# A state-space scan kernel: some input products moved from VectorE and GpSimd to ScalarE, with a transpose by TensorE, and the steps' side work placed by tables

## The chip, the cores and the metric

The kernel runs on one NeuronCore of a Trainium2 chip. The core has five engines that run side by side, each through its own queue in order: TensorE (PE in the profile; its weight loads are PEld), VectorE (DVE), ScalarE (ACT), GpSimd (POOL) and SyncE (SP), which only issues DMAs here. Tiles lie in SBUF or in PSUM[...]. The metric is the time of one execution in microseconds (us), the median of three runs.

## What is computed

Four layers in one launch; only layers 0 and 1 contain the work that changes. Each is a selective state-space scan over images of 56 x 56 positions, in four directions (by rows, by columns, and both backwards). For each direction, channel and state n of 16, with the position i running in order:

```
def step(state, inp):
    u_i, d_i, b_i, c_i = inp
    dA = jnp.exp(d_i[..., None] * A)
    state = dA * state + (d_i * u_i)[..., None] * b_i[:, :, None, :]
    y = jnp.einsum('bkdn,bkn->bkd', state, c_i)
    return (state, y)
```

So for a state n the kernel needs a decay exp(delta * A[n]), an input product (delta * u) * B[n], in which B[n] is one row of numbers shared by all channels, a recurrence along the positions, a product with the row C[n], and the sum of these products over the 16 states. Layer 0 has two images one after the other with 256 channels (two halves of 128); layer 1 has both images side by side on 128 partitions (64 channels each) and goes through four heads one after the other, each needing the one before. Layers 2 and 3 (attention, a long convolution, a mixture of experts) follow and are not touched.

## The kernel before

The 3136 positions are cut into four pieces of 784 (`QT`). A *group* is one direction and one piece; there are 16 in a scan run. A *step* s is one state of one group and one half of the channels: in layer 0 a group has 2 x 16 steps, in layer 1 16. Layer 0 has two runs of 512 steps, layer 1 four of 256, so there are 2048 steps. Between the runs lie stages with norms, projections and convolutions.

One step uses every engine, on tiles of 128 x 784:

- `decay` (L339): ScalarE writes `a` = exp(A[n] * delta) into one of two PSUM slots (`pdec0`, `pdec1`, by the parity of s). A slot is free when the scan two steps earlier has read it.
- The input product. For 11 of 16 states (*direct* below), `spread` (L364) lets TensorE copy the row B[n] to all 128 partitions of a PSUM tile `b`, of which there is one, and VectorE multiplies it by `du` = delta * u (L417). For the five states in `POOLED` (2, 5, 8, 11, 14) the row comes by a broadcast DMA (`on_all`, L299) and GpSimd multiplies (L433).
- `scan` (L358): one VectorE instruction, h = a * h + input along the 784 positions, in place in `h`; from the second piece of a direction on it starts from a carried state, which `keep` (L350) copies out on ScalarE.
- GpSimd multiplies `h` by the row C[n], which comes by a broadcast DMA (L430, result `p`).
- `add_up` (L378): TensorE adds `p` to the group's PSUM sum `acc` with two matmuls; `take_out` (L398) copies the full sum to `y` on ScalarE in the third step of the next 16.

All of it is written out by hand: `emit(s)` issues the pieces of several steps in one fixed order, so that in iteration s the scan of step s, the decay and product of step s+1, the spread of s+2, the DMA for C of s+3 and the sum of step s-2 stand together. The queues keep that order:

```
        if one:
            self.decay(one)
```

Beside the steps runs the *preparation* of the next group (`pieces_of`): `rows` (projection on TensorE, copied by ScalarE), `keep`, `fetch`, `band`, `rest`, `store` and `spread` (the rows of B go through DRAM and are split into three bf16 parts, `rest` on GpSimd L195), `steps` and `soft` (delta, with a change of the activation table), `copy` and `times` (du; L223 on VectorE). A list gives each piece an iteration and a place in it. Pieces of place 0 use the same single PSUM tile `b` (pool `prow`) as `spread`. `first` does the preparation of a run's first group in the stage before the run.

## Time and profile before

| what | value |
|---|---|
| time, median of three runs | 9113.85 us (9098.83 to 9114.19) |
| span of the profiled execution | 9096.6 us |
| its six scan runs together | 5060.4 us |
| VectorE busy over the span | 7088.0 us, 78% |
| GpSimd busy over the span | 6350.1 us, 70% |
| ScalarE busy over the span | 3854.8 us, 42% |
| TensorE busy over the span | 7993.2 us, 88% (pipelined, not a measure of its peak) |

The page gives no time of the profiled execution other than its span; the three runs lie from 2 to 17 us above it. In a group's row, "L358 DVE ... x1536 | 2791.8, 1840 | 51.6 <-ACT a L339 28.7" means: line 358 of the kernel, on VectorE, 1536 instructions, busy 2791.8 us in all and 1840 ns each, and VectorE was idle for 51.6 us just before them, 28.7 of it until ScalarE had written `a`. Shares over the whole span mix stages with different limits, so the scan runs are best read by themselves. In a row of stretches, each engine's busy time stands ahead of its number of instructions, and the last three columns are TensorE's granted clock (1 is full), the share of the DMA engines' time and the bandwidth.

### The profile page before, as it was taken

To read this page: it belongs to the slowest core of one execution; us is meant where nothing else is said; L and a number is where in the kernel's file an instruction comes from. 1 tells how busy PE (TensorE), PEld (TensorE's weight loads), DVE (VectorE), ACT (ScalarE), POOL (GpSimd) and SP (SyncE) were. 2 spreads that over 40 slices of the span, in tenths; PEclk is the share of its full clock that TensorE was granted. 3 is DMA by queue.
4 is the path that set the end of the run, shared out by engine and by line. 5 is a ranking of instruction groups with operands and counts; after the bars stand their busy time and mean duration, and the time that the engine had idled before them with its cause. 6 is when DMAs were issued, how large, how long until landed. Compare 5 with 4: busy or idle time off the path is not lost. (4 is left out here: it accounts for less than half of the span.)

```text
span 9096.6 us, 93496 instructions
## 1 busy us (share of the span) xinstructions
PE 7993.2 (88%) x28687; PEld 4765.5 (52%) x28687; DVE 7088.0 (78%) x7568; ACT 3854.8 (42%) x6644; POOL 6350.1 (70%) x4066
## 2 busy tenths in 40 slices
PE   8888888888887888888888888699999999999998
PEld 4444445444444444444444444355688888874555
DVE  8999998999997997998999899511467667665442
ACT  4555545555555555554554555433211111114331
POOL 6999996999996997998899799566311111115551
PEclk9999999999999998998999899799999999999999
DMA  5666664666664995996898699100233333320004
GB/s 159 221 221 220 222 212 127 221 221 220 222 220 110 230 226 134 227 228 157 203 227 204 157 227 224 39 3 3 85 96 105 104 94 110 93 63 8 14 1 135
DMA packets 780368, 1362.92 MB, mean 150 GB/s; under 512 B 133101, under 2 KB 405486, under 8 KB 779834
## 3 DMA queue, kind: packets, MB, share of 16 engines
q1 hardware_dynamic: 779866, 1356.95, 53.1%
q8 instruction: 227, 3.72, 0.2%
q14 instruction: 275, 2.25, 0.1%
HBM read 1317.03 MB, written 39.60 MB: 149 GB/s over the span
## 5 line engine op out<-in xcount | busy, mean ns | idle before, releaser
L430 POOL TENSOR_TENSOR p<-h,c 128x784 f32<-128x784 f32 x2048 | 3761.2, 1864 | 115.0 <-DVE h L358 33.1
L358 DVE TENSOR_TENSOR_SCAN h<-a,state,h 128x784 f32<-128x784 f32 x1536 | 2791.8, 1840 | 51.6 <-ACT a L339 28.7
L378 PE MATMUL acc<-p,center 128*128 128x392 f32 x4096 | 1499.0, 499 | 22.7 <-POOL p L430 20.8
L378 PE MATMUL acc<-p,ident 128*128 128x392 f32 x4096 | 1491.9, 498 | 6.7 <-POOL p L430 6.7
L417 DVE TENSOR_TENSOR h<-du,b 128x784 f32<-128x784 f32 x1408 | 1336.7, 949 | 75.6 <-PE b L364 70.4
L339 ACT ACTIVATE a<-delta,L0A 128x784 f32<-128x784 f32 x1024 | 939.3, 918 | 973.4 <-DVE h L358 971.5
L339 ACT ACTIVATE a<-delta,L1A 128x784 f32<-128x784 f32 x1024 | 939.2, 917 | 908.3 <-DVE h L358 905.3
L364 PE MATMUL b<-three,sel 96*128 96x512 bf16 (+1 forms) x2816 | 728.6, 341 | 563.9 <-DVE h L417 460.1
L433 POOL TENSOR_TENSOR h<-du,b 128x784 f32<-128x784 f32 x640 | 1190.3, 1860 | 4.1 <-PE pcv L460 4.1
L378 PEld LDWEIGHTS acc<-p,center 128*128 128x128 f32 x4096 | 740.9, 192 | 536.8 <-POOL p L430 60.2
L378 PEld LDWEIGHTS acc<-p,ident 128*128 128x128 f32 x4096 | 743.9, 192 | 512.8 <-POOL p L430 26.5
L1089 POOL TENSOR_TENSOR total<-total,e 128x448 f32<-128x448 f32 (+1 forms) x644 | 735.6, 1142 | 326.0 <-ACT e L1078 286.0
L358 DVE TENSOR_TENSOR_SCAN h<-a,h 128x784 f32<-128x784 f32 x512 | 901.7, 1780 | 36.7 <-ACT a L339 21.1
L364 PEld LDWEIGHTS <-sel 96*128 96x128 bf16 x2816 | 281.5, 100 | 1230.9 <-issue 1048.6
L1572 DVE TENSOR_TENSOR u<-u,cv 128x512 f32<-128x512 f32 x1024 | 623.7, 681 | 326.6 <-PE cv L1559 325.4
L1603 POOL TENSOR_TENSOR u<-u,S 128x1024 f32<-128x1024 f32 x64 | 150.0, 2365 | 1041.0 <-DVE S L1572 1041.0
L1078 ACT ACTIVATE e<-sc 128x448 f32<-128x448 f32 (+1 forms) x700 | 377.2, 543 | 723.0 <-PE sc L1076 596.3
L1574 ACT COPY u<-cv 128x512 f32<-128x512 f32 x256 | 149.5, 587 | 829.3 <-PE cv L1559 775.7
L1673 PE MATMUL pj<-u,Wm 128*128 128x196 f32 (+8 forms) x1536 | 354.7, 384 | 5.7 <-DVE A L1679 5.7
L1076 PE MATMUL sc<-big 128*128 128x448 f32 (+1 forms) x700 | 323.4, 547 | 15.4 <-ACT e L1078 12.3
L1070 PE MATMUL av<-e,big 128*128 128x448 f32 (+1 forms) x700 | 320.9, 545 | 1.2 <-DVE e L1083 1.0
L1653 POOL TENSOR_TENSOR both<-mpm 128x512 f32<-128x512 f32 x32 | 40.6, 1269 | 392.3 <-DVE Wm L1709 272.8
(452 smaller groups left out, 11251.1 us busy)
## 6 DMA issues: line engine op xcount, KB each, us to landing
c<-rows SPq DMA_DIRECT2D x1024, 392.0 KB, 4.0
c<-rows SPq DMA_DIRECT2D x2048, 196.0 KB, 4.8
b<-rows SPq DMA_DIRECT2D x320, 392.0 KB, 4.5
b<-rows SPq DMA_DIRECT2D x640, 196.0 KB, 4.6
H<-raw SPq DMA_DIRECT2D x32, 1568.0 KB, 7.6
wC<-win SPq DMA_DIRECT2D x64, 576.0 KB, 6.4
w<-in_L_weight_dram SPq DMA_DIRECT2D x52, 512.0 KB, 6.3
wA<-win SPq DMA_DIRECT2D x64, 384.0 KB, 5.6
```

The source lines that it names most:

```text
L339: self.k.nc.scalar.activation(x["a"], g["delta"][ci], AF.Exp, scale=self.w["A"](g["kd"], ci, x["n"]))
L358: self.k.nc.vector.tensor_tensor_scan(h, a, h, start, ALU.mult, ALU.add)
L364: self.k.nc.tensor.matmul(ps[:, c0:c1], lhsT=self.w["selB"](x["n"]), rhs=x["g"]["three"][:, c0:c1], start=True, stop=True)
L378: nc.tensor.matmul(job["acc"][:, i, 0:392], lhsT=self.w["sum"], rhs=x["p"][:, 392 * i : 392 * (i + 1)], start=False, stop=n == NS - 1,)
L417: nc.vector.tensor_tensor(one["h"], one["g"]["du"][one["ci"]], one["b"], ALU.mult)
L430: nc.gpsimd.tensor_tensor(now["p"], now["h"], now["c"], ALU.mult)
L433: nc.gpsimd.tensor_tensor(three["h"], three["g"]["du"][three["ci"]], three["b"], ALU.mult)
L1076: nc.tensor.matmul(ps[:n], lhsT=keys[b][:, KT * j : KT * j + n], rhs=q, start=True, stop=True)
L1078: nc.scalar.activation(e[:n], ps[:n], AF.Exp, scale=scale)
L1089: nc.gpsimd.tensor_tensor(total[:n], total[:n], e[:n], ALU.add)
L1572: nc.vector.tensor_tensor(place(o), place(o), ps, ALU.add)
L1673: nc.tensor.matmul(ps[:, lo - c0 : hi - c0], lhsT=Ws[f][:, eo, r, :], rhs=u[:, b, f, lo - a0 : hi - a0], start=f == 0, stop=f == 1,)
```

## The change

A third way to make the input product joins the two. For *turned* states (1, 5, 7, 11, 13 in layer 0; 3 and 11 in layer 1) ScalarE works on transposed tiles. The group's `du` is transposed once (`turn`: seven tiles of 112 positions by 128 channels, through PSUM, into `duT`), and so are the rows of B (`across`, into `BT`). With positions on the partitions, B[n] is one number per partition, so a `fan` is an activation Copy of one 112 x 128 tile with a scale per partition; seven of them make a state's product in layer 0, 14 of 64 columns in layer 1, where the two images have rows of their own. `back` lets TensorE transpose the seven tiles into the PSUM slot that the decay would have used, and the decay of a turned state goes to an `h` tile in SBUF instead; the scan then reads `a` from SBUF and the product from PSUM, and writes `h` over `a`.

Fewer states are pooled (3, 9, 15 in layer 0; 1, 6, 9, 14 in layer 1), and 8 (layer 0) or 10 (layer 1) stay direct. `copy` becomes a ScalarE copy into PSUM in place of a TensorE product with the identity. Tables now say in which iteration each fan (`fans`, by the six iterations before the scan), each sum (`adds`, how many per iteration) and each preparation piece (`lists`, with `short` while the first group of layer 1 runs) is issued. The transposed tiles lie in memory that is otherwise idle in the runs; for that, layer 1's `hT` becomes a small rotating tile.

```diff
-POOLED = (2, 5, 8, 11, 14)
 HALF = QT // 2
+TS = QT // TP
...
+        self.pooled, self.turned = w["pooled"], w["turned"]
+        self.duT, self.bT = w["turn"][0:2], w["turn"][2:]
...
+                i = len(self.groups)
+                self.groups.append(dict(
+                    kd=kd, q=q, step=step, back=back,
+                    duT=[self.duT[(i * self.nch + ci) % 2] for ci in range(self.nch)],
+                ))
...
-            g["copy"] = product(ps, [0, 1], lambda m: k.ident, [xq[ci]])
+            g["copy"] = ps[:, :, 0:HALF]
+            nc.scalar.copy(g["copy"], part(xq[ci], [0, 1]))
...
+        def transposed(out, of, n, tiles, ps):
+            ps = ps.rearrange("p i c -> p (i c)")[:TP]
+            for i, j in enumerate(tiles):
+                nc.tensor.transpose(ps[:, n * i : n * (i + 1)], of[0:n, TP * j : TP * (j + 1)], k.ident[0:n, 0:n])
+            nc.scalar.copy(
+                out[:, tiles[0] : tiles[-1] + 1], ps[:, 0 : n * len(tiles)].rearrange("p (i c) -> p i c", c=n)
+            )
+
+        def across(ps):
+            g["BT"] = once("BT", 32 * TS)[:TP]
+            transposed(g["BT"].rearrange("p (i c) -> p i c", c=32), g["xd"], 32, range(TS), ps)
+
+        def turn(ci, ps, tiles=range(TS)):
+            transposed(g["duT"][ci], g["du"][ci], 128, tiles, ps)
...
+        f["across"](ps())
+        for ci in range(self.nch):
+            for i in range(0, TS, 3):
+                f["turn"](ci, ps(), range(i, min(i + 3, TS)))
...
-        def bands(keep, fetch, band, apart, store, spread):
-            yield from ((keep, 2, "keep"), (fetch, 2, "fetch"), (store, 2, "store"), (spread, 2, "spread"))
-            for i in range(3):
-                yield band + apart * i, 2, "band", i
...
+        lists = self.w["short"] if short and self.nch == 1 else self.w["lists"]
...
+        self.fans, self.adds = {}, self.w["adds"]
+        for i, x in enumerate(x for x in steps if x["n"] in self.turned):
+            x["bT"] = self.bT[i % len(self.bT)]
+            todo = [(x, j, *part) for j in range(TS) for part in self.w["parts"]]
+            at = self.w["fans"]
+            for j, count in enumerate(at.get(x["s"] % 32, at[None])):
+                self.fans.setdefault(x["s"] - 6 + j, []).extend(todo[:count])
+                todo = todo[count:]
...
-            if place == 0:
+            if place < 2:
...
+    def fan(self, x, i, c0, c1, row):
+
+
+        g, r = x["g"], 32 * i + row + x["n"]
+        self.k.nc.scalar.activation(
+            x["bT"][:, i, c0:c1], g["duT"][x["ci"]][:, i, c0:c1], AF.Copy, scale=g["BT"][:, r : r + 1]
+        )
+
+    def slot(self, x, at=0):
+        return self.pa[x["s"] % 2].tile([128, 1024], F32, name=f"a{x['s'] % 2}")[:, at : at + QT]
+
+    def back(self, x):
+
+        x["b"] = self.slot(x, 512 - 4 * TP)
+        for i in range(TS):
+            self.k.nc.tensor.transpose(x["b"][:, TP * i : TP * (i + 1)], x["bT"][:, i, :], self.k.ident[:TP, :TP])
+
+    def direct(self, x):
+        return x["n"] not in self.pooled and x["n"] not in self.turned
+
     def decay(self, x):
         g, ci = x["g"], x["ci"]
-        x["a"] = self.pa[x["s"] % 2].tile([128, 1024], F32, name=f"a{x['s'] % 2}")[:, 0:QT]
+        if x["n"] in self.turned:
+            x["a"] = x["h"] = self.hp.tile([128, QT], F32, name="h")
+        else:
+            x["a"] = self.slot(x)
...
         self.k.nc.scalar.activation(x["a"], g["delta"][ci], AF.Exp, scale=self.w["A"](g["kd"], ci, x["n"]))
...
+        b = x["b"] if n in self.turned else h
         start = 0.0 if g["step"] == 0 else self.state[g["kd"], g["step"] - 1, ci][:, n : n + 1]
         if g["back"]:
-            a, h = a[:, ::-1], h[:, ::-1]
-        self.k.nc.vector.tensor_tensor_scan(h, a, h, start, ALU.mult, ALU.add)
+            a, h, b = a[:, ::-1], h[:, ::-1], b[:, ::-1]
+        self.k.nc.vector.tensor_tensor_scan(h, a, b, start, ALU.mult, ALU.add)
...
+    def add(self, s):
+        for _ in range(self.adds[s % len(self.adds)]):
+            if self.sums and "acc" in self.sums[0]["job"]:
+                self.add_up(self.sums.pop(0))
...
+        if done:
+            self.sums.append(done)
...
-        if one:
+        if one and one["n"] not in self.turned:
             self.decay(one)
...
+        if two and two["n"] in self.turned:
+            self.decay(two)
+        for args in self.fans.get(s, ()):
+            self.fan(*args)
+        if one and one["n"] in self.turned:
+            self.back(one)
+        self.prepare(s, 1)
+        if one and self.direct(one):
             one["h"] = self.hp.tile([128, QT], F32, name="h")
             nc.vector.tensor_tensor(one["h"], one["g"]["du"][one["ci"]], one["b"], ALU.mult)
-        if two and two["n"] not in POOLED:
+        if two and self.direct(two):
             self.spread(two)
+        soon = self.w["soon"] and (s, 0) in self.pieces
+        if soon:
+            self.add(s)
...
         self.prepare(s, 0)
         if now:
...
-        if done:
-            self.sums.append(done)
-            if done["n"] == 2:
-                self.begin_sum(done["job"])
-            elif done["n"] > 2:
-                for _ in range(2 if done["n"] in (6, 9, 12) else 1):
-                    self.add_up(self.sums.pop(0))
+        if done and done["n"] == 2:
+            self.begin_sum(done["job"])
+        if not soon:
+            self.add(s)
...
+                "parts": ((0, 128, 0),),
+                "pooled": (3, 9, 15),
+                "turned": (1, 5, 7, 11, 13),
+                "adds": (0, 2, 0, 0, 0, 1, 1, 2, 1, 1, 1, 0, 1, 1, 2, 0, 3, 0, 2, 0, 1, 0, 2, 1, 2, 1, 0, 1, 2, 1, 1, 2),
+                "soon": True,
+                "fans": {
+                    None: (0, 2, 2, 2, 1, 0),
+                    1: (0, 2, 2, 1, 2, 0),
+                    5: (2, 3, 2, 0, 0, 0),
+                    7: (0, 0, 0, 7, 0, 0),
+                    11: (1, 3, 3, 0, 0, 0),
+                    13: (3, 3, 0, 1, 0, 0),
+                    17: (0, 2, 1, 3, 1, 0),
+                    21: (0, 3, 3, 1, 0, 0),
+                    23: (3, 4, 0, 0, 0, 0),
+                    27: (0, 0, 1, 2, 0, 4),
+                    29: (0, 0, 0, 5, 2, 0),
+                },
+                "lists": [
+                    [
+                        (1, 0, "rows", [0]), (3, 0, "rows", [1]), (3, 2, "keep"), (5, 0, "across"),
+                        (5, 2, "fetch"), (8, 2, "band", 0), (8, 2, "rest", 0), (10, 2, "band", 1),
+                        (10, 2, "rest", 1), (11, 0, "steps", 0, [0, 1]), (15, 0, "steps", 1, [0, 1]),
+                        (18, 2, "band", 2), (21, 2, "soft", 0), (21, 2, "soft", 1), (23, 2, "store"),
+                        (25, 2, "spread"), (25, 0, "copy", 0), (25, 2, "times", 0), (27, 0, "turn", 0),
+                        (29, 0, "copy", 1), (29, 2, "times", 1), (41, 0, "turn", 1),
+                    ],
+                ],
+                "turn": [X[:, TS * i : TS * (i + 1), 1, :] for i in range(4)],
...
+            "parts": ((0, 64, 0), (64, 128, NS)),
+            "pooled": (1, 6, 9, 14),
+            "turned": (3, 11),
+            "adds": (0, 2, 2, 0, 0, 1, 2, 1, 1, 1, 1, 2, 1, 1, 1, 0, 3, 1, 0, 0, 0, 1, 2, 1, 1, 1, 2, 0, 1, 1, 1, 1),
+            "soon": False,
+            "fans": {
+                None: (0, 4, 4, 4, 2, 0),
+                3: (0, 10, 4, 0, 0, 0),
+                11: (4, 0, 1, 7, 2, 0),
+                19: (4, 5, 5, 0, 0, 0),
+                27: (5, 1, 3, 2, 3, 0),
+            },
+            "lists": [
+                [
+                    (1, 0, "rows", [0, 1]), (2, 2, "keep"), (4, 0, "steps", 0, [0, 1]), (5, 2, "fetch"),
+                    (9, 0, "across"), (9, 2, "band", 0), (9, 2, "rest", 0), (10, 2, "band", 1),
+                    (10, 2, "rest", 1), (11, 2, "band", 2), (17, 2, "soft", 0), (19, 2, "store"),
+                    (22, 2, "spread"), (23, 0, "copy", 0), (23, 2, "times", 0), (25, 0, "turn", 0),
+                ],
+                [
+                    (12, 0, "rows", [0, 1]), (14, 2, "keep"), (15, 0, "steps", 0, [0, 1]), (17, 2, "soft", 0),
+                    (19, 2, "fetch"), (20, 0, "across"), (27, 2, "band", 0), (27, 2, "rest", 0),
+                    (28, 0, "copy", 0), (28, 2, "times", 0), (29, 2, "band", 1), (29, 2, "rest", 1),
+                    (31, 2, "band", 2), (33, 2, "store"), (35, 2, "spread"), (39, 0, "turn", 0),
+                ],
+            ],
+            "short": [
+                [
+                    (1, 0, "rows", [0, 1]), (4, 2, "keep"), (4, 0, "steps", 0, [0, 1]), (5, 2, "fetch"),
+                    (6, 2, "soft", 0), (7, 0, "across"), (7, 2, "band", 0), (7, 2, "rest", 0),
+                    (7, 2, "times", 0, False), (8, 2, "band", 1), (8, 2, "rest", 1), (9, 2, "band", 2),
+                    (9, 2, "store"), (10, 2, "spread"), (12, 0, "turn", 0),
+                ],
...
+            "turn": [
+                big[5][:TP, 128 * TS * i : 128 * TS * (i + 1)].rearrange("p (i c) -> p i c", c=128) for i in range(3)
+            ],
...
-            nc.scalar.copy(self.hT[:, cs], pt)
+            hT = sp.tile([2 * D, CH], F32, name="hT")
+            nc.scalar.copy(hT, pt)
             ps = vp.tile([128, CH], F32, name="pcv")
-            nc.tensor.matmul(ps, lhsT=W["in_w"][:, 0, :], rhs=self.hT[:, cs], start=True, stop=True)
+            nc.tensor.matmul(ps, lhsT=W["in_w"][:, 0, :], rhs=hT, start=True, stop=True)
```

## The prediction

> **What bounds it now.** I read the page's groups first, then the stretches of the six scan runs, then a few microseconds of VectorE and GpSimd in order of time. A scan run here goes from its first to its last scan.
>
> From the page (span; then busy us, mean ns, idle before and its releaser):
>
> ```profile
> span 9096.6 us, 93496 instructions
> ...
> L430 POOL TENSOR_TENSOR p<-h,c 128x784 f32<-128x784 f32 x2048 | 3761.2, 1864 | 115.0 <-DVE h L358 33.1
> L358 DVE TENSOR_TENSOR_SCAN h<-a,state,h 128x784 f32<-128x784 f32 x1536 | 2791.8, 1840 | 51.6 <-ACT a L339 28.7
> L417 DVE TENSOR_TENSOR h<-du,b 128x784 f32<-128x784 f32 x1408 | 1336.7, 949 | 75.6 <-PE b L364 70.4
> L433 POOL TENSOR_TENSOR h<-du,b 128x784 f32<-128x784 f32 x640 | 1190.3, 1860 | 4.1 <-PE pcv L460 4.1
> ```
>
> The six scan runs (two of 512 states in layer 0, four of 256 in layer 1):
>
> ```profile
> core 0: us, PE busy (x) PEld busy (x) DVE busy (x) ACT busy (x) POOL busy (x), PEclk, DMA share, GB/s
> 102.50:1359.20 1256.70, 1049.90 (x3224) 534.27 (x3224) 1227.40 (x892) 655.00 (x1122) 1230.48 (x700) 0.96 0.68 219
> 1490.90:2748.70 1257.80, 1051.52 (x3224) 535.03 (x3224) 1227.64 (x894) 655.73 (x1122) 1230.74 (x701) 0.96 0.69 221
> 2883.70:3519.50 635.80, 526.20 (x1605) 265.26 (x1606) 613.12 (x446) 338.05 (x583) 620.33 (x365) 0.95 0.90 226
> 3615.90:4248.90 633.00, 523.48 (x1605) 264.04 (x1606) 612.78 (x446) 338.04 (x583) 621.48 (x366) 0.96 0.91 224
> 4345.60:4983.40 637.80, 528.19 (x1604) 266.68 (x1604) 613.33 (x446) 338.07 (x583) 621.21 (x366) 0.95 0.89 223
> 5079.70:5719.00 639.30, 528.06 (x1604) 265.13 (x1604) 614.05 (x447) 338.35 (x583) 621.22 (x367) 0.95 0.89 222
> ```
>
> VectorE and GpSimd are both 96 to 98% busy in every run; ScalarE only 53%. The runs hold 5060 us of the span; per 16 states they take 39.28 us in layer 0 (2514.5/64) and 39.78 us in layer 1 (2545.9/64). Busy times overlap at their ends, so I take the pitch from the timeline:
>
> ```profile
> 415.38 1.85 DVE L358 TENSOR_TENSOR_SCAN h<-a,state,h 128x784 f32<-128x784 f32 x1
> 417.14 0.95 DVE L417 TENSOR_TENSOR h<-du,b 128x784 f32<-128x784 f32 x1
> 418.00 3.47 DVE L358 TENSOR_TENSOR_SCAN h<-a,h 128x784 f32<-128x784 f32 x2
> ...
> 422.37 1.78 DVE L358 TENSOR_TENSOR_SCAN h<-a,h 128x784 f32<-128x784 f32 x1
> 424.07 0.95 DVE L417 TENSOR_TENSOR h<-du,b 128x784 f32<-128x784 f32 x1
> ```
>
> ```profile
> 421.10 5.49 POOL L430 TENSOR_TENSOR p<-h,c 128x784 f32<-128x784 f32 x3
> 426.54 1.85 POOL L433 TENSOR_TENSOR h<-du,b 128x784 f32<-128x784 f32 x1
> 428.34 5.51 POOL L430 TENSOR_TENSOR p<-h,c 128x784 f32<-128x784 f32 x3
> ```
>
> Start to start: a scan with carried state 1.76 us, without 1.70; three quarters carry one, so 1.745. VectorE's product 0.86 (L417), `times` 0.89 (L223). GpSimd: 1.805 for either product, a `rest` about 0.52. So, per 16 states:
> - VectorE, both layers: 16 x 1.745 + 11 x 0.86 + 0.89 = 38.3.
> - GpSimd: 21 x 1.805 = 37.9, with one `rest` in layer 0 38.4, with two in layer 1 38.9.
>
> The two are level, and the measured 39.28 and 39.78 stand 0.9 above. Of that, L417's wait for PE's `b` is 70.4/128 = 0.55: a preparation piece had taken the one PSUM buffer that the spread needs.
>
> [...] Here each scan and product of VectorE has one PSUM input, and the pitches above stand while GpSimd is 98% busy[...]. The turned scan keeps that: `a` moves to SBUF, but `b` to PSUM. [...]
>
> **The change, part by part.** Per 16 states:
>
> *VectorE.* Layer 0: 11 products become 8, 16 x 1.745 + 6.9 + 0.9 = 35.7 (from 38.3). Layer 1: 10 remain, 37.4. A turned scan reads `a` in SBUF, `b` in PSUM; no row shows that form. The operands only trade places, so I take 1.745; bounds -0.05 to +0.1 us, over 448 turned scans -22 to +45 us.
>
> *GpSimd.* Layer 0: pooled 5 to 3, 19 x 1.805 + 0.5 = 34.8. Layer 1: 5 to 4, 20 x 1.805 + 1.0 = 37.1. Two `b` broadcasts fall away in layer 0, one in layer 1, so DMA eases.
>
> *ScalarE.* A scaled copy exists already in the final norm, same shape and operand kind:
>
> ```profile
> 5744.54 2.45 ACT L89 ACTIVATE X<-X,stf 112x128 f32<-112x128 f32 x8
> ```
>
> With 0.39 for the last (the median of one such copy), (2.45 - 0.39)/7 = 0.295 us each. Layer 0: 5 x 7 = 35 copies, 10.3 us. [...] 2 x 14 = 28 copies, 6.7 us. `turn`'s 896 columns (estimate 0.9), `across` (0.1 to 0.3) and `copy`, which leaves TensorE (estimate 0.85): 1.9 to 2.1. Sum, from 655.0/32 = 20.5: layer 0 32.7 of about 36; layer 1 from 338/16 = 21.1: 29.9 of about 38. All of it hides under VectorE if none is late. The tightest place I find is the seven copies for state 7: counting from the end of scan 2, with decays at 0.85 (L339's 0.918 less its overlap), ScalarE does decay 4 (to 1.05), the take-out's two copies (2.2), a state copy and decay 5 (3.15), `rows` (3.6), another state copy and seven scaled copies (5.75), decay 6 (6.6); scan 6 wants it at 1.745 x 3 + 0.86 x 2 = 6.95. Spare: 0.35 us.
>
> *TensorE.* Seven transposes for each turned state; the trace's nearest:
>
> ```profile
> 2801.49 0.57 PE L852 MATMUL pt<-ident,nrm 112*64 112x112 f32 x4 [2.19 <-POOL nrm L86]
> ```
>
> With 0.26 for one, (0.57 - 0.26)/3 = 0.10 us each. These load 64 weight columns, the new ones 128, so I bound them above by 0.19, as if the whole step were doubled. Seven: 0.7 us. `back` for s+1 waits until scan s-1 leaves its PSUM slot, and the spread for s+2 (0.34 us) stands behind it. Together with about 0.3 of latency this ends 1.3 us after scan s-1; the product of s+2 wants it after scan s, at 1.745. Cover: 0.45 us. One state in 32 has its last four copies right at `back`; there `times` (0.89) delays the product too, which leaves about 0.3.
>
> *What queues behind the new waits.* On TensorE the spread and then the sums stand behind `back`; VectorE's product waits for the spread. On ScalarE a scaled copy waits for its `bT` tile, freed by the `back` of two turned states earlier in layer 0 and one earlier in layer 1, at least a step before; behind it stands the next decay, for which VectorE's scan waits.
>
> *Pieces and sums.* In layer 0 every TensorE piece now falls on an odd step, in layer 1 on one whose state s+2 is pooled or turned, so none stands between a spread and its product. Most of the 0.55 should go. Six sum buffers and six `h` buffers remain, and each product of GpSimd finds its sum done at least one step before. On SP `fetch` waits for `keep` and `spread` for `store` with two or more steps between (one at the short start), against a broadcast that lands in 4.0 to 4.8 us and is issued three steps ahead: no cost, up to 2 us a group if uncovered.
>
> *Outside.* `first` gains 7 + 7 transposes and up to seven copies per run; `hT` becomes a rotating tile. Six runs at 0 to 3 us: +10.
>
> **Sum.** I leave 0.6 of waiting in layer 0 (36.3) and 0.8 in layer 1 (38.2), where VectorE and GpSimd are level again. Layer 0: 64 x 36.3 = 2323, -191. Layer 1: 64 x 38.2 = 2445, -101. With +10: span 8815. The runs shown lie 2 to 17 us above the profiled span (median 9113.85), so 8830.
>
> **Rivals.** (1) *Partial gain*: GpSimd still bounds layer 1, or ScalarE's FIFO comes late a few times per 32 states. For it: ScalarE at 90%, spare of 0.35 us, GpSimd at 37.1. Against: the DMA and piece waits shrink. Layer 1 unchanged, layer 0 at 37.5: -114, about 9000. (2) *Slower*: the spread behind `back` on TensorE comes late at every turned state. The gain of 292 us over 448 turned states is 0.65 us; beyond the cover of 0.45, that is copies ending 1.1 us after scan s-1, or transposes and spreads at half clock (1.3 + 0.67 + 0.3 = 2.3, late by 0.55) with a little more. At 1.0 us late: 8815 + 448, about 9270. For it: no buffer lets `back` start earlier. Against: granted clock 0.95 or more in every run, and copies that end a step ahead. (3) *No effect*: something else holds 39 us. No engine or queue does (DMA 0.69 and 0.9, easing), so 0.02.
>
> **Numbers.** Chances: likeliest 0.66, partial 0.22, same 0.02, slower 0.10. Own range of the likeliest: 8750 (no waiting: 35.7 and 37.4 give -382) to 8910. The range runs on to 9000 and leaves out some 0.05 below and 0.15 above. Within 0.2% counts as the same (18 us), about what three runs can tell.
>
> **What will show it.** Right: stretches near 1162 and 611 us, scan groups of 1.75 us pitch with L417's successor at 1152 instructions, VectorE at 98%, scaled copies at 0.29. Wrong: VectorE idle before its product with PE's `b` as releaser (rival 2), before the scan with ScalarE's `a` (rival 1), a turned scan above 1.9 us, or GpSimd idle on DMA.

## The result, and the profile after

The changed kernel takes 9007.29 us (median of 4 runs, 8996.70 to 9012.54), the kernel before in the same comparison 9106.34 (4 runs, 9092.49 to 9114.19): a ratio of 0.989 [0.9876, 0.9904]. It is faster by 99 us where 284 were forecast; the time lies 7 us above the range and where the first rival, the partial gain, put it. Whether that rival's reasons were the ones, the experiments tell.

The page of the kernel after, with the groups that answer to those shown of before (busy us, mean ns, idle before and its releaser), and the two of the running sums on TensorE:

```profile
span 9010.8 us, 104738 instructions
...
L492 POOL TENSOR_TENSOR p<-h,c 128x784 f32<-128x784 f32 x2048 | 3763.8, 1863 | 293.8 <-DVE h L401 147.7
L401 DVE TENSOR_TENSOR_SCAN h<-a,state,h 128x784 f32<-128x784 f32 x1200 | 2169.4, 1832 | 2.9 <-ACT a L381 2.3
L421 PE MATMUL acc<-p,center 128*128 128x392 f32 x4096 | 1491.6, 500 | 6.0 <-POOL p L492 5.9
L421 PE MATMUL acc<-p,ident 128*128 128x392 f32 x4096 | 1431.0, 493 | 0.5 <-POOL p L492 0.4
L476 DVE TENSOR_TENSOR h<-du,b 128x784 f32<-128x784 f32 x1152 | 1095.4, 951 | 233.1 <-PE b L407 211.2
...
L401 DVE TENSOR_TENSOR_SCAN h<-h,state,a 128x784 f32<-128x784 f32 x336 | 617.6, 1838 | 0.0
```

Three things stand in it. A turned scan costs what the other form costs (1838 against 1832 ns). GpSimd now waits (293.8 us, 115.0 before), so it is no longer the bound in either layer. And the waits of VectorE have moved to one place: nothing to speak of before its scans (51.6 before), but 233.1 us before its product, nearly all of it with TensorE's spread `b` as releaser (75.6 before). Two rows of 4096 matmuls each are the sums of 2048 states: four records to a state. The prediction never counted them.

The stretches of the scan runs in layer 0, and the first two of layer 1:

```profile
core 0: us, PE busy (x) PEld busy (x) DVE busy (x) ACT busy (x) POOL busy (x), PEclk, DMA share, GB/s
108.80:1290.00 1181.20, 1101.10 (x4345) 623.95 (x4346) 1144.04 (x797) 1013.84 (x2312) 1121.83 (x637) 0.99 0.67 212
1434.10:2617.90 1183.80, 1104.70 (x4345) 626.54 (x4343) 1144.09 (x798) 1010.99 (x2304) 1122.07 (x637) 0.98 0.67 213
2766.00:3403.80 637.80, 544.51 (x1952) 294.22 (x1951) 604.48 (x430) 461.25 (x1060) 594.28 (x349) 0.95 0.78 216
3508.70:4144.60 635.90, 542.56 (x1952) 293.53 (x1951) 604.15 (x430) 461.47 (x1060) 594.74 (x349) 0.96 0.78 213
```

Layer 0 fell from 2514.5 to 2365.0 us (1181.2 + 1183.8), which is 36.95 for 16 states. Layer 1 did not fall: its four runs take 637.8, 635.9, 639.2 and 639.0, together 2551.9 against 2545.9, although VectorE's work in each is 9 us less. TensorE is now 93% busy in layer 0 (1101.10 of 1181.20), where it was 84% (1049.90 of 1256.70).

Outside the runs more was lost than forecast. The stretch between the first two runs of layer 1, before and after:

```profile
3519.50:3615.90 96.40, 84.40 (x302) 53.76 (x302) 49.94 (x111) 49.34 (x81) 45.00 (x50) 0.73 0.14 32
```

```profile
3403.80:3508.70 104.90, 90.75 (x311) 56.38 (x311) 49.06 (x110) 55.93 (x101) 44.18 (x51) 0.69 0.11 29
```

All six stretches ahead of a run sum to 715.6 us, before to 658.6: +57 instead of +10. (In the traces of `short_apart`, `sum_later`, `row_begin` and `no_fans` below, which leave these stretches as they are, they sum to 715.0, 701.4, 702.8 and 697.4, so the loss is 39 to 57 us.) What follows the last scan is the same (3378.3 and 3377.6).

So the prediction's span of 8815 was missed by 196 us: 42 in layer 0 (2365 for 2323), 107 in layer 1 (2552 for 2445), 47 outside the runs. Taking VectorE's waits in the runs, without `times`, from its records, after has 82 us in layer 0 and 157 in layer 1, where the prediction left 38 and 51. Steps are counted below in sets of 32, and a wait "at step 21" is one that follows scan 21 of a set. Divided by place, and now with `times` (0.88 each) in the count: the first 32 steps of each run of layer 1 wait 18 to 21 us (8 to 10 before). In layer 0 the half of each run that goes by rows went down from 29 to 22 or 23 us, the half that goes by columns up from 27.5 to 41.

What stands ahead of a late product in layer 1, in order of time (start us, duration, idle before; VectorE's and TensorE's lines and one of ScalarE's):

```profile
3058.87 0.94 DVE L476 TENSOR_TENSOR h<-du,b 128x784 f32<-128x784 f32 x1
...
3059.73 3.58 DVE L401 TENSOR_TENSOR_SCAN h<-a,state,h 128x784 f32<-128x784 f32 x2
...
3059.87 2.98 PE L173 MATMUL b<-xd,dt 128*128 128x392 f32 x4 [2.13 <-DVE h L476]
...
3062.64 1.65 PE L435 MATMUL acc<-big,ident 128*128 128x392 f32 x4
...
3062.89 0.91 ACT L218 ACTIVATE delta<-b,L1dtb 128x784 f32<-128x784 f32 x1 [2.93 <-PE b L173]
...
3064.13 0.50 PE L407 MATMUL b<-three,sel 96*128 96x512 bf16 x2
...
3064.73 0.97 DVE L476 TENSOR_TENSOR h<-du,b 128x784 f32<-128x784 f32 x1 [1.42 <-PE b L407]
```

TensorE, idle for 2.13 us, starts the four records of a `steps` piece as soon as the PSUM slot `b` is free, at half clock (0.50 granted in those 2.98 us). `begin_sum` stands behind it, and ScalarE must first empty the slot (to 3063.80). Only then comes the spread, and VectorE, whose second scan ended at 3063.31, starts the product 1.42 us late.

At the start of a run two such pieces stand in a row (VectorE and TensorE of the second run of layer 1; the clock granted to both pieces is 0.50):

```profile
3511.26 3.46 DVE L401 TENSOR_TENSOR_SCAN h<-a,h 128x784 f32<-128x784 f32 x2
3520.26 0.97 DVE L476 TENSOR_TENSOR h<-du,b 128x784 f32<-128x784 f32 x1 [5.54 <-PE b L407]
```

```profile
3511.40 2.98 PE L173 MATMUL b<-big,xp 128*128 128x392 f32 x4 [2.19 <-DVE h L476]
3515.28 2.98 PE L173 MATMUL b<-big,xp 128*128 128x392 f32 x4 [0.90 <-ACT xd L185]
3518.05 1.51 PE L370 MATMUL a<-ident,big 112*128 112x112 f32 x7
3519.36 0.86 PE L407 MATMUL b<-three,sel 96*128 96x512 bf16 x2
```

The list `short` puts `rows` of both following groups at step 1 (and `steps` of both at step 4); VectorE waits 5.54 us there.

### The profile page after: what moved, and what is told of

Its sections match the earlier page's. It is cut to its first block, busy times and chain, and to the rows that moved or that the text cites. A ratio compares the mean times of both kernels' runs of the same rounds, so it can differ in the third digit from the quotient of the medians.

```text
span 9010.8 us, 104738 instructions
## 1 busy us (share of the span) xinstructions
PE 8222.8 (91%) x32399; PEld 5096.0 (57%) x32399; DVE 6874.5 (76%) x7312; ACT 5097.6 (57%) x11031; POOL 6021.1 (67%) x3874
## 5 line engine op out<-in xcount | busy, mean ns | idle before, releaser
L492 POOL TENSOR_TENSOR p<-h,c 128x784 f32<-128x784 f32 x2048 | 3763.8, 1863 | 293.8 <-DVE h L401 147.7
L401 DVE TENSOR_TENSOR_SCAN h<-a,state,h 128x784 f32<-128x784 f32 x1200 | 2169.4, 1832 | 2.9 <-ACT a L381 2.3
L476 DVE TENSOR_TENSOR h<-du,b 128x784 f32<-128x784 f32 x1152 | 1095.4, 951 | 233.1 <-PE b L407 211.2
L381 ACT ACTIVATE a<-delta,L1A 128x784 f32<-128x784 f32 x896 | 819.8, 915 | 423.4 <-DVE h L401 418.8
L495 POOL TENSOR_TENSOR h<-du,b 128x784 f32<-128x784 f32 x448 | 831.7, 1856 | 0.0
L407 PE MATMUL b<-three,sel 96*128 96x512 bf16 (+1 forms) x2304 | 587.5, 336 | 181.4 <-DVE h L476 110.2
L381 ACT ACTIVATE a<-delta,L0A 128x784 f32<-128x784 f32 x704 | 643.2, 914 | 170.3 <-DVE h L401 165.6
L401 DVE TENSOR_TENSOR_SCAN h<-a,h 128x784 f32<-128x784 f32 x400 | 702.4, 1773 | 3.4 <-ACT a L381 3.1
L359 ACT ACTIVATE X<-X,BT 112x128 f32<-112x128 f32 x2100 | 683.8, 391 | 0.2
L401 DVE TENSOR_TENSOR_SCAN h<-h,state,a 128x784 f32<-128x784 f32 x336 | 617.6, 1838 | 0.0
L359 ACT ACTIVATE big<-big,BT 112x64 f32<-112x64 f32 x1680 | 444.6, 335 | 0.0
L370 PE MATMUL a<-ident,X 112*128 112x112 f32 x2240 | 292.7, 269 | 83.5 <-DVE h L401 76.2
```

The costliest lines, as they stand in the source:

```text
L359: self.k.nc.scalar.activation(x["bT"][:, i, c0:c1], g["duT"][x["ci"]][:, i, c0:c1], AF.Copy, scale=g["BT"][:, r : r + 1])
L370: self.k.nc.tensor.transpose(x["b"][:, TP * i : TP * (i + 1)], x["bT"][:, i, :], self.k.ident[:TP, :TP])
L381: self.k.nc.scalar.activation(x["a"], g["delta"][ci], AF.Exp, scale=self.w["A"](g["kd"], ci, x["n"]))
L401: self.k.nc.vector.tensor_tensor_scan(h, a, b, start, ALU.mult, ALU.add)
L407: self.k.nc.tensor.matmul(ps[:, c0:c1], lhsT=self.w["selB"](x["n"]), rhs=x["g"]["three"][:, c0:c1], start=True, stop=True)
L476: nc.vector.tensor_tensor(one["h"], one["g"]["du"][one["ci"]], one["b"], ALU.mult)
```

## Experiments: the start of a run

Theory A: the loss outside the runs is the place of the first group's `across` and `turn`, which stand in the queues behind chunk 2 and ahead of the next chunks; the loss at the start of a run is two groups' pieces at one step. Its rival: both are time that the work costs wherever it stands. The first experiment issues `across` and `turn` behind chunk 5.

```
             f["times"](ci, False)
+        self.rest_of_first = f
+
+    def first_turn(self, pool):
+        f = self.rest_of_first
...
         f["across"](ps())
...
         if c == 2:
             self.scans.first(vp)
+        if c == 5:
+            self.scans.first_turn(vp)
...
```

> The changed kernel, with the first group's across and turn moved in the stage before a run from behind chunk 2 to behind chunk 5. Theory A (TensorE's queue: the new transposes wait there for du, and the stage's convolutions stand behind them): the six stretches between the runs, 715.6 us in the changed kernel against 658.6 before, fall to about 675, so the time falls by about 40 us to 8967, ratio to the kernel before 0.985. Theory B (ScalarE's added copies make the stage longer): the same copies are still there, no change, 0.989.

It took 8955.12 us, 0.9825 [0.9809, 0.9842]. The stretches ahead of the runs sum to 657.4, as before the change (658.6), while the runs stay at 2359.3 and 2555.4. Theory A holds: the loss was the place and not the work. In the trace of after, the first group's transposes in layer 1 run 69.2 to 71.6 us into the stretch, since they need `du`, and the last convolution ends at 103.8; before the change it ended at 95.1.

The second parts the two groups in layer 1's list for the start of a run: the second one's `rows` go from step 1 to 9, `steps` from 4 to 15.

```
 "short": [
     [
-        (1, 0, "rows", [0, 1]), (4, 2, "keep"), (4, 0, "steps", 0, [0, 1]), (5, 2, "fetch"),
+        (1, 0, "rows", [0, 1]), (2, 2, "keep"), (4, 0, "steps", 0, [0, 1]), (4, 2, "fetch"),
...
     [
-        (1, 0, "rows", [0, 1]), (1, 2, "keep"), (4, 0, "steps", 0, [0, 1]), (6, 2, "soft", 0),
-        (7, 0, "across"), (10, 2, "fetch"), (14, 2, "band", 0), (14, 2, "rest", 0),
+        (9, 0, "rows", [0, 1]), (10, 2, "keep"), (15, 0, "steps", 0, [0, 1]), (17, 2, "soft", 0),
+        (12, 2, "fetch"), (20, 0, "across"), (15, 2, "band", 0), (15, 2, "rest", 0),
```

> The changed kernel, with the two groups that are prepared at the start of a layer 1 run set apart: the second one's rows at iteration 9 in place of 1, its steps at 15 in place of 4, its soft at 17 in place of 6 (one more change of the activation table). Theory A (two pieces in one iteration keep the single tile b from the spreads): the first 32 steps of each of four runs give back about 8 of the 10.6 us that they lost, about -32 us, ratio 0.9855. Theory B (ScalarE late): one more table change makes it 0 to 10 us longer, 0.989 to 0.990.

8973.81 us, 0.985 [0.9835, 0.9865]. Layer 1 fell from 2551.9 to 2529.0, and the waits of its first 32 steps from 19.7 to 12.4 us a run. Part of that 107 is therefore the doubled start, some 23 to 29 us of it.

The two together:

> Complete in its work: the changed kernel with across and turn behind chunk 5 (turn_later) and layer 1's short start set apart (short_apart), layer 1's other lists as changed. If the two causes are separate, their gains add: 9007 less 52 less 33 = about 8922, ratio to the kernel before 0.979 (sum of the two measured ratios' gains: 1 - 0.0065 - 0.004 below 0.989 = 0.9785). If they share a cause (TensorE's clock at the start of a run), less: 0.982.

8929.07 us, 0.9802 [0.9789, 0.9815]; stretches 652.4, layer 1 2530.2, layer 0 2359.4. The gains add, to within 7 us of the 8922 expected.

## Experiments: where the wait of a piece goes

In the steady part of layer 1 the largest wait stands at step 21 (1.72 us on average over the sets), with 0.58 at step 5 and 0.53 at 18. Steps 5 and 21 come just after a piece and `begin_sum`, step 18 just after a piece. The average hides that step 21 waits in some sets and not in others. The late product shown above is one of its waits. In another set of the same trace the step goes like this:

```profile
3727.03 1.58 PE L173 MATMUL b<-xd,dt 128*128 128x392 f32 x4 [2.13 <-DVE h L476]
...
3730.40 0.94 DVE L476 TENSOR_TENSOR h<-du,b 128x784 f32<-128x784 f32 x1
```

The pause ahead of the piece is the same 2.13 us, but the piece runs at full clock (1.00 granted, 1.58 us), and VectorE does not wait. A `steps` piece stands at this place in 24 sets. In 5 of them (all in the half by rows) it takes 1.58 us at a granted clock of 1.00, and none of the 5 waits. In the other 19 (7 by rows, 12 by columns) it takes 2.08 to 2.98 us at a granted clock of 0.73 to 0.50, and all of them wait, 1.42 to 3.06 us, 46 us in all. So the wait at step 21 goes with TensorE's clock in this kernel. `begin_sum` counts as well: in the trace of `both` below, nine such pieces run at full clock in the half by columns, with a `begin_sum` of 3.05 us behind them, and each of these waits 1.46 us. No experiment below holds the clock still.

The next three move a piece or `begin_sum`. First `begin_sum` alone, from the third to the fourth state of a channel block:

```
-        if done and done["n"] == 2:
+        if done and done["n"] == self.w["begin"]:
             self.begin_sum(done["job"])
...
+            "begin": 3,
             "pooled": (1, 6, 9, 14),
```

> The changed kernel, with layer 1's begin_sum one iteration later, behind the spread of state 7 in TensorE's queue in place of ahead of it. Theory A (the spread is late because of what TensorE has ahead of it): the wait between scans 21 and 22 of a 32-step set falls from 1.7 us to about 0.4 and the one between 5 and 6 from 0.6 to 0; over 28 steady sets about -40 us, ratio 0.985. Theory B (the spread waits for ScalarE to empty b, begin_sum lies beside that): 0, 0.989.

9038.22 us, 0.992 [0.9905, 0.9934]: slower than the change as it stands, and both theories' numbers miss. The wait at 5 went and that at 21 fell to 1.06, but 1.46 came up at 22, 0.87 at 6 and 0.65 at 24; layer 1 rose to 2594.7. Part of the wait went where `begin_sum` went.

Then the pieces, on top of the two edits of `both`: the first group's `steps` goes from 4 to 7, and the second's `across` from 20 to 17, so that no step has both a piece and `begin_sum`.

```
...
-    (1, 0, "rows", [0, 1]), (2, 2, "keep"), (4, 0, "steps", 0, [0, 1]), (5, 2, "fetch"),
+    (1, 0, "rows", [0, 1]), (2, 2, "keep"), (7, 0, "steps", 0, [0, 1]), (5, 2, "fetch"),
...
-    (19, 2, "fetch"), (20, 0, "across"), (27, 2, "band", 0), (27, 2, "rest", 0),
+    (19, 2, "fetch"), (17, 0, "across"), (27, 2, "band", 0), (27, 2, "rest", 0),
...
```

> Complete in its work: across and turn behind chunk 5 (as turn_later), the short start set apart (as short_apart), and in layer 1 the first group's steps at iteration 7 in place of 4 and the second group's across at 17 in place of 20, so that neither stands with begin_sum. TensorE theory: -52 and -33 us as measured for the first two, and another 20 to 35 from the waits at steps 21 and 5 of the steady sets: about 8890, ratio 0.976. ScalarE theory: no more than the first two, 0.9785.

8988.92 us, 0.9859 [0.9845, 0.9874], 60 us above `both`. The wait at 21 is gone, and 2.66 us stand at 24; layer 1 takes 2582.7. But iteration 7 was not free: the second group's `turn` stands at 39 in its list, which is iteration 7 of the next set. Two lines of this run at that step:

```profile
3788.84 1.58 PE L173 MATMUL b<-xd,dt 128*128 128x392 f32 x4 [0.99 <-ACT big L237]
...
3792.18 0.97 DVE L484 TENSOR_TENSOR h<-du,b 128x784 f32<-128x784 f32 x1 [3.85 <-PE b L415]
```

Two pieces go through the one tile `b`, and TensorE stands idle for 0.99 us until ScalarE has copied the first out of it. The other way, on top of `both`, the first group's `rows` goes to -1 and its `steps` to 1:

```
...
-    (1, 0, "rows", [0, 1]), (2, 2, "keep"), (4, 0, "steps", 0, [0, 1]), (5, 2, "fetch"),
+    (-1, 0, "rows", [0, 1]), (0, 2, "keep"), (1, 0, "steps", 0, [0, 1]), (5, 2, "fetch"),
...
```

> As both, with layer 1's first-group rows at iteration -1 in place of 1 and its steps at 1 in place of 4, so that neither stands in the iteration of begin_sum or in the one with two direct states in a row. TensorE theory: the wait after scan 21 (1.7 to 2.2 us in 32) falls below 0.5 and none over 1 us takes its place: -30 to -50 us against both, ratio 0.975. If a piece costs VectorE its wait wherever it stands (as the mended run's did, 2.7 us after scan 24), no gain: 0.979 or more.

8951.06 us, 0.9823 [0.981, 0.9837]. Again the wait at 21 is gone and another stands in its place: 18 rose from 0.53 to 2.51. There the piece, at full clock, stands behind the three sums that the table `adds` gives to the iteration before it (12 records, 4.11 us), and one more sum and a `back` stand between it and the spread. Three moves in layer 1's steady part, and each moved the wait. The places that the pieces went to were taken, by `turn` in one case and by three sums in the other, so the moves do not show that the queue has no room anywhere; a free place was not tried.

## Experiments: what fills TensorE

Adding up TensorE's records for a set of 32 steps of layer 0 gives the sum that the prediction did not make. Each f32 matmul of 392 columns leaves two records, each 0.33 us after the other when nothing interrupts. A state's sum has two matmuls: 4 x 0.33 = 1.31 us, 42 us for 32 states. Spreads take 5.4, `back` 7, `rows` and `steps` 2.6 each, `turn` and `across` 2, `begin_sum` 2.6 in the half by rows and 5.8 in the half by columns. That is 64 to 67 us of the 72.6 that the prediction left for 32 steps, and it must be served in order. Before the change it was 60 to 63 of 78.6.

The total alone does not make the wait, though. In layer 0's half by rows, with the 64, VectorE waits less than before the change (22 or 23 us for 29). In layer 1, where the wait grew most, the same figures give an estimate of 62 to 65 us of the 76.4 that the prediction left, and TensorE is 85% busy (544.51 of 637.80), against 93% in layer 0. What counts, as far as the traces show, is what stands ahead of one spread and how long it takes there.

The long `begin_sum` of the columns is a matter of how `y` is read. In column order neighbouring columns of the operand lie 56 elements apart. Two of this instruction's lines in the kernel after, that of layer 0 and that of the direction read in order (duration in ns, lowest/median/highest; `skip` is the direction that starts from `row`, read in order):

```profile
L435 PE MATMUL acc<-pair,ident x192: 490/902/966, 411.9 to 2594.8; 128*128 128x392 f32 x192
...
L435 PE MATMUL acc<-big,skip x128: 490/492/861, 121.7 to 5138.9; 128*128 128x392 f32 x128
```

Theory T: VectorE waits in the columns' half because this instruction is long. Rival: the columns' half waits for its loads or for ScalarE. The experiment reads `y` in row order there; the addition of what the other directions left is then wrong in the groups by columns, and nothing is left out.

```
-                lhsT, rhs = self.k.ident, self.y_half(job, i)
+                lhsT, rhs = self.k.ident, self.y_half(dict(job, g=dict(job["g"], kd=0)), i)
```

> The changed kernel, but begin_sum reads the y of the groups by columns in row order (contiguous, so other positions are added: this part of the result is left wrong). In the traces one record of begin_sum takes 0.90 us by columns and 0.49 by rows, pitch 0.72 and 0.33, four records a group. TensorE theory (what stands ahead of the spread in TensorE's queue makes VectorE wait): the second half of each run (the columns) falls to the waits of the first: about 19 us in each layer 0 run, 5 to 10 in each layer 1 run, -55 to -60 in all, ratio to the kernel before 0.983. ScalarE theory (late scaled copies): nothing, 0.989.

8952.84 us, 0.9818 [0.9802, 0.9834]. Layer 0 fell to 2333.0: the columns' half from 40.8 to 28.1 and 26.7 us, with the waits at steps 6 and 22 (about 1.4 and 1.0 us on average there) gone. Layer 1 fell by 10, to 2541.8. Theory T holds for layer 0, and with this layer 0 stands 10 us from its forecast. For layer 1 the 10 us are not the whole share of `begin_sum`: in this run all 24 `steps` pieces at step 21 took over 2.4 us, at half clock in whole or in part, and the wait there rose to about 2.2 us.

The largest term, the sums themselves, was to be tested by leaving half of it out: only the first 392 of 784 columns of each `p` are summed.

```
-        for i in range(2):
+        for i in range(1):
             nc.tensor.matmul(
                 job["acc"][:, i, 0:392], lhsT=self.w["sum"], rhs=x["p"][:, 392 * i : 392 * (i + 1)],
...
```

> The changed kernel, with only the first half of each product p summed over the states (the second halves' 2 of 4 TensorE records per state are left out, 0.65 us a state). TensorE theory (its queue is nearly full: four records of 0.33 for each state's sum alone are 21 us of the 37 us for 16 states): most of VectorE's waits for b go, layer 0 to about 36.0 us for 16 states, layer 1's steady part to 37.7, -110 to -150 us in all, ratio 0.974. ScalarE theory: nothing, 0.989.

9087.35 us, 0.9965 [0.9953, 0.9976]: slower than with all the sums, by any theory the wrong side. The list of cores (span, mean granted clock of TensorE) shows what else changed:

```profile
core 0: 9087.2 us, clock 0.890
```

After has 0.954. With less to do TensorE was granted the half clock more often: spreads whose second record takes over 0.36 us (277 ns at the median; in after those over 0.36 have a granted clock of 0.50) went from 13 to 88 in layer 0 and from 26 to 161 in layer 1, and VectorE's next product needs each of them. That this makes the whole loss is argued and not shown. Nor is it shown what makes the clock fall. In the trace of after TensorE's last pauses do not tell it: the `steps` piece at 3059.87 runs at half clock (0.50 granted) after a pause of 2.13 us, with others of 0.81 and 1.06 in the 12 us ahead of it; the piece at 3727.03, at full clock (1.00), has 2.13, 1.06 and 0.75 ahead of it. So this run can't tell what half of the sums is worth at a constant clock, and that number stays open.

Less drastic, the TensorE part of `rows` and `steps` in the runs is left out; ScalarE copies another operand from SBUF instead, so these pieces no longer use the tile `b` either.

```
...
+            if ps is None:
+                nc.scalar.copy(part(g["xd"], halves), part(xq[0], halves))
+                return
...
-            r = product(ps, halves, lambda _: w["dt"](kd, ci), [g["xd"]])
+            r = part(g["xd"], halves) if ps is None else product(ps, halves, lambda _: w["dt"](kd, ci), [g["xd"]])
...
-            if place < 2:
+            if f.__name__ in ("rows", "steps"):
+                f(*args, None)
+            elif place < 2:
...
```

> The changed kernel with the TensorE half of rows and steps left out in the scan runs (ScalarE copies other SBUF data in their place, so the decays are of other numbers): they no longer take the tile b nor TensorE's time. TensorE and tile b theory: layer 1's waits after scans 5, 18 and 21 go, its steady 32 steps fall from 4.8 us of waits (times 1.76 among them) to about 2, the start of its runs by another 8 us each, layer 0 by 0.6 in 32: -120 to -140 us, ratio 0.975. If TensorE's clock falls for want of work, as in half_sums, less than half of that.

8977.25 us, 0.9853 [0.9839, 0.9866]. Layer 1 fell by 46 us to 2505.7, its first 32 steps from 19.7 to 11.8 us of waits; layer 0 rose by 23, to 2387.7, with 1.54 at step 6 where 0.75 stood; the mean clock was 0.941. The gain is less than half of what theory T said, and the clock fell as in `half_sums`, less far. Leaving out the two kinds of piece is worth 46 us to layer 1 at the clock of this run. The run cannot tell the pieces' time on TensorE from their use of the one tile `b`; a second tile was not tried.

## Experiments: the other suspects

ScalarE, the first rival's engine: all scaled copies but those of the first four turned states of each run are left out (the turned products are stale).

```
-            todo = [(x, j, *part) for j in range(TS) for part in self.w["parts"]]
+            todo = [(x, j, *part) for j in range(TS) for part in self.w["parts"]] if i < 4 else []
```

> The changed kernel, with the scaled copies left out after the first four turned states of each run (TensorE goes on transposing what then lies there). ScalarE loses about 10 us for 16 states in layer 0 and 7 in layer 1. ScalarE theory (VectorE waits because copies, and what ScalarE has behind them, are late): -80 us or more, ratio 0.980 or less. TensorE theory: back never waits for a copy, little more: 0 to -20 us, ratio 0.987 to 0.989.

9004.29 us, 0.9877 [0.986, 0.9893]: the same as with them. 3752 scaled copies of 4032 are gone (ScalarE has 7279 instructions instead of 11031), and layer 1 stands at 2548.9, layer 0 at 2358.9. The scaled copies on ScalarE are not what the gain was lost to.

And the change in layer 0 alone, with layer 1's lists as they were:

```
-            "pooled": (1, 6, 9, 14),
-            "turned": (3, 11),
+            "pooled": (2, 5, 8, 11, 14),
+            "turned": (),
...
```

> Layer 1 as before the change (five pooled states, no turned ones, the old lists and sums, copy by TensorE), layer 0 as changed. If layer 1's part of the change is worth nothing or less: its four runs take about 2546 us as before in place of 2552, the stretches ahead of three of them fall back by 8 to 9 us each and the one behind layer 0 by some 8, so about -40 us, 8967, ratio 0.985. If layer 1 gains in its steady state what the prediction gave it (1.6 us in 16 states), the time rises by 60 us or more, ratio 0.996.

8980.11 us, 0.9856 [0.9841, 0.9871], 27 us below the whole change. Layer 1's runs take 2547.6, level with the 2551.9 of after, and the stretches ahead of them fall from 104.9 to 95 to 97 us. As it stood, the change bought nothing in layer 1's runs and cost its stretches.

Last, a version made of what held: `both`, and `begin_sum` of the columns that walks its elements in the other order. It reads `y` in runs of seven neighbours and writes PSUM with a stride of 56 instead; each element goes where it went.

```
+            out = job["acc"][:, i, 0:392].rearrange("p (a b) -> p a b", b=HW)
+            if g["kd"] % 2 == 1:
+                out, rhs = out.rearrange("p a b -> p b a"), rhs.rearrange("p a b -> p b a")
+            self.k.nc.tensor.matmul(out, lhsT=lhsT, rhs=rhs, start=True, stop=False)
-            self.k.nc.tensor.matmul(
-                job["acc"][:, i, 0:392].rearrange("p (a b) -> p a b", b=HW), lhsT=lhsT, rhs=rhs, start=True, stop=False
-            )
```

> Complete in its work: as both, and begin_sum of the column groups walks its 392 elements in the other order: y is read in runs of 7 neighbours and the sum's PSUM tile is written with a stride of 56, where before y was read with a stride of 56 and the tile written in order. If the stride of TensorE's moving operand makes a record's pitch 0.72 us and begin_sum's length makes VectorE wait (row_begin): pitch back to 0.33 to 0.45, layer 0's second halves lose 12 to 19 us of waits each, -25 to -45 us against both in all, 8890, ratio to the kernel before 0.976. If the stride in PSUM costs as much as the one in SBUF, no change: 0.980.

8894.65 us, 0.9764 [0.9751, 0.9778]: better than both kernels. The same instruction, in this kernel:

```profile
L446 PE MATMUL acc<-pair,ident x192: 489/493/862, 409.1 to 2552.1; 128*128 128x392 f32 x192
```

and VectorE's product:

```profile
L485 DVE TENSOR_TENSOR h<-du,b 128x784 f32<-128x784 f32 x1152 | 1095.7, 951 | 163.4 <-PE b L415 154.6
```

The wait before the product is down from 233.1 to 163.4 us, layer 0 takes 2333.0 and layer 1 2523.2.

## Why the prediction was wrong

**Bound and VectorE's work: right.** The kernel was held by VectorE and GpSimd level; taking 4 and 1 products of 16 from them made room. The turned form at 1.745 us, the open number, was right (1838 against 1832 ns mean, with GpSimd 95% busy in layer 0's runs, 1121.83 of 1181.20); whether the one operand in PSUM that both forms have matters there was not shown. The wait before scans with a carried state fell from 51.6 to 2.9 us.

**The chain for a turned state: right.** The transposes and the spread behind them end 1.42 us after the scan where nothing else is ahead of them, for a forecast of 1.3 and a limit of 1.745: a spread that ended at 634.58 us, behind a scan whose successor began at 633.16, with no wait. Of the 1.42 us, 0.23 pass before the first transpose, 0.69 to the spread (the transposes start 0.096 apart at the median, for 0.10 and a bound of 0.19) and 0.50 in it; the forecast's 0.3 of latency was the author's estimate. The second rival, which priced this chain as late at every turned state, did not happen. Its sign did come, VectorE idle before its product with TensorE's `b` as releaser (211.2 us), but from other work ahead of the spread.

**ScalarE: right in price, right that it is hidden.** Scaled copies come 0.29 us apart (391 ns busy), for a forecast of 0.295. Those of 64 columns come 0.24 apart (335), 6.7 us for 28; the same 6.7 in the prediction was the author's estimate. Its figures for the copies of `turn`, `across` and `copy` (0.9, 0.1 to 0.3 and 0.85) were estimates too; they take 0.89, 0.34 and 0.80. In all ScalarE is busy for 31.7 us per 16 states in layer 0 (1013.84/32) and 28.8 in layer 1 (461.25/16), for 32.7 and 29.9. The first rival named the time but not the cause: `no_fans` rules out the scaled copies on ScalarE, and GpSimd waits 293.8 us. That its 9000 us came so close is luck: it had 114 us of gain in layer 0 and nothing else, and the runs show 150 in layer 0, 6 lost in layer 1 and 57 lost outside.

**"Pieces and sums" and the "0.6" and "0.8" of waiting: this step failed.** It asked only whether a piece stands between a spread and its product, and let most of the old wait go. It put no time on what stands on TensorE ahead of the next spread. The wait grew instead, from 75.6 to 233.1 us. TensorE was counted as one chain per turned state, never as a queue with a sum, which in layer 0 takes 64 to 67 us of the 72.6. A `begin_sum` by columns of 2.9 us, or a piece of 1.3 to 3 us, delays the next spread when it stands ahead of it. Shown: in layer 0, `begin_sum` by columns makes 26 to 32 of the 42 us (26 from `both` to `both_order`, 32 in `row_begin`). In layer 1, of 107 us, `short_apart` shows 23 as two groups' pieces at once, and `no_pieces` 46 as all `rows` and `steps`, these included; `begin_sum` by columns is 7 to 10 more. The other half of layer 1's 107 was not isolated, and its cause stays open. The trace points at TensorE's clock, since in the changed kernel every wait of step 21 has its piece at half clock in whole or in part (0.50 to 0.73 granted); the one tile `b` and the sums are the other candidates, and no run separates them.

**"Outside: +10": failed in size.** The seven transposes and copies were priced by their own time, 0 to 3 us a run. They cost 39 to 57 because they wait for `du` in the middle of the queues and the next chunks' convolutions stand behind them; `turn_later` gets all of it back with the same work.

**The sum for layer 1.** With no wait it was to give 2394 and the forecast 2445; it stayed at 2552: VectorE's work fell by 9 us a run, and its waits grew by a little more. `l0_only` shows that the change as it stood was worth making in layer 0 alone; with the start of its runs mended (`both`), layer 1 takes 2530.2, 16 us less than before the change.

## What to carry to other kernels

When work moves off the two busiest engines, go through every in-order queue that it moves to, not just the chain that is being built. Add it up, and then look, step by step, at what stands ahead of the one instruction that the busiest engine waits for, and at which clock it runs: here one long `begin_sum`, or one piece at half clock (2.98 us for 1.58), was a wait. Work placed in the run-up to a loop is priced by what it waits for and what queues behind it; some 40 to 57 us went to a few microseconds of transposes issued three chunks early. And a cheap thing to look at in a full TensorE is the order in which its moving operand is read: here 902 or 493 ns a record.

## What the runs showed of the hardware that was not expected

- An f32 matmul of 392 columns leaves two records of 0.33 us pitch each; read with neighbouring columns 56 elements apart, each takes 0.72 (902 against 492 ns busy). The same elements read in runs of seven and written to PSUM 56 apart take 493 (in layer 1's runs 597 at the median).
- Less work on TensorE made the kernel slower: with half of the sums left out, its mean clock fell from 0.954 to 0.890 and the time rose by 80 us. TensorE's pauses of the last 12 us do not tell the clock: with the same 2.13 and 1.06 us ahead of it, the same piece took 1.58 us in 5 sets and 2.08 to 2.98 in 19. Here `half_sums` and `no_pieces` (mean clock 0.941), which took work from TensorE, changed two things at once, and their times are read only together with the clock.
